# A 32-head attention's product with Wo for two token tiles at once, by seven products of sums of blocks in place of eight

## The chip, the cores and the metric

The program runs on one NeuronCore of a Trainium2 chip. TensorE (PE) multiplies matrices and writes to PSUM; VectorE (DVE), ScalarE (ACT) and GpSimd (POOL) work on tiles of 128 partitions in SBUF, the first two also on PSUM; SyncE (SP) issues the DMAs. Each engine works through its own instructions in a fixed order and waits on semaphores for the others. The metric is the device time of one execution in microseconds; less is better.

## What is computed

A block of four decoder layers on 16 x 64 tokens of width 512, in float32. Each layer adds a cross attention and a feed-forward part to x. The change is in the attention of layer 1, which has 32 query heads of width 128 and 8 key/value heads:

```python
x = x + _L0_xattn_ref(_layernorm(x, axis=-1), ctx_4096, ...)
x = x + _L0_ffn_ref(_layernorm(x, axis=-1), ...)
x = x + _L1_xattn_ref(_layernorm(x, axis=-1), ctx_4096, ...)
...
def _L1_xattn_ref(latents, context, Wq, Wk, Wv, Wo, q_norm_w, k_norm_w):
    kv = jnp.concatenate([context, latents], axis=1)
    q = (latents @ Wq).reshape(bsz, q_len, HEADS, HEAD_DIM).transpose(0, 2, 1, 3)
    k = (kv @ Wk).reshape(bsz, kv_len, KV_HEADS, HEAD_DIM).transpose(0, 2, 1, 3)
    v = (kv @ Wv).reshape(bsz, kv_len, KV_HEADS, HEAD_DIM).transpose(0, 2, 1, 3)
    q = rms_norm(q, q_norm_w)
    k = rms_norm(k, k_norm_w)
    ...
    probs = jax.nn.softmax(scores.astype(jnp.float32), axis=-1).astype(q.dtype)
    out = jnp.einsum('bhgqk,bhkd->bhgqd', probs, v)
    ...
    return out @ Wo
```

Wo is 4096 x 512. Taken by key/value head, its share is 512 x 512: four query heads of 128 rows each.

## The kernel before

**Tokens, groups, heads.** The 1024 tokens are eight tiles of 128. `groups` pairs them: (0,1), (2,3), (4,5), (6,7). x stays in SBUF for the whole program, a 128x512 tile for each token tile.

**Two lanes on one TensorE.** `decoder_kernel` writes two streams of steps and `merged` weaves them. The main lane (a) runs layer 1's attention, `normed_attention`, for all four groups, and then the rest for tiles 4 to 7. The side lane (b) runs layer 0 (window attention and an int8 FFN) for one group after the other, ahead of the main lane, and then the rest for tiles 0 to 3. Each step yields a cost in microseconds; after a main step the side lane is advanced until it has used that cost times a rate (0.85 for the first group, then 0.78, 0.78, 0.74). A `Need` makes the main lane wait, in the order of writing, until the side lane has passed a mark. TensorE runs in exactly the order written (`manual_schedule`); the order on the other engines is made by the compiler. A side step may contain no matmul at all.

**The attention as a pipeline.** `normed_attention` first makes the keys and values of the context for all heads and saves them in DRAM. Then `ticks` walks over 64 units: a unit is u = (n, t), with n = 8 x group + key/value head and t one of the group's two tiles, so that the two tiles of a head are neighbours. In tick i every step is run, in the order of the list, on the unit that lies its lag behind:

```python
(2, scores, 0.9),
(1, scale, 0.0),
(5, project, 3.4),
(0, queries, 3.4),
(1, turn, 0.7),
(0, keys_values, 1.7),
(4, values, 0.9),
(3, turn_weights, 0.4),
```

`queries` (L857) makes a unit's four query heads, `keys_values` (L875) its own keys and values, whose squares are reduced on VectorE to r, raised to the power -1/2 on GpSimd (L123). `scale` (L898) and `turn` make normed, transposed queries and keys; `scores` (L672) the products, their maximum on VectorE (L682), the exponentials on ScalarE (L688), and p divided by its sum on GpSimd (L697). `turn_weights` transposes p (copied out of PSUM on VectorE, L704), and `values` (L713) multiplies by v; ScalarE copies the result to aT, 128 x (four heads x 128 tokens) (L927). `project` multiplies the four 128x128 pieces of aT by the four 128x512 pieces of the head's Wo, adds them up in one PSUM bank (L722), and VectorE adds that bank to x (L157).

**Weights.** Head n's Wo piece, 1 MB, is loaded by `out_weights` (L761) from `queries` of head n+2, into one of two buffers of tag "o"; the buffers serve the context's key and value weights before that (`pair_weights`). The rest of the head's weights, 1.5 MB, is another load (L752).

**PSUM.** Each lane has four banks in rotation. A tick of the attention takes eight: scores, project, queries, two in `turn`, keys_values, values, turn_weights.

**The window attention of the side lane.** For each pair of tiles, `output` forms sixteen products of weights and values on VectorE (pv, L466), whose weights come by DMA from DRAM, 512 KB each (att, tag "prod"), and adds them up on GpSimd (acc, L476); it has no matmul. Its result goes into a product on TensorE (ps_o, L321).

## Time and profile before

| | us |
|---|---|
| three runs | 1639.91, 1640.31, 1640.88 (median 1640.31) |
| span of the profiled execution | 1642.0 |
| first attention unit's Wo product, last one's | 224.6, 1109.4 |
| Wo product of layer 1, TensorE busy (512 matmul instructions) | 231.1 |
| queries of layer 1, TensorE busy (512) | 233.0 |
| keys and values of layer 1, TensorE busy (512) | 125.0 |
| Wo loads, issue to landing, median (32 of 1024 KB) | 5.2 |
| transfers in all | 200.32 MB, 122 GB/s over the span |

TensorE was granted 0.993 of its full clock. The three runs lie within 0.97 us, and the profiled execution's span is 1.7 us above their median. In the profile a float32 product appears as two matmul instructions. Times of single instructions are in microseconds from the span's start; a row of a timeline gives start, length, engine, line, operation, what is written and read, shapes and how many instructions are merged in the row; brackets give idle time before it and what ended it. In the groups, the number after the bar is the time in which the engine was busy with them, then the mean length of one in ns, then the idle time before them.

### The profile page before, as it was taken

What the parts mean: (1) busy time and instruction counts of PE and PEld (TensorE: products, weight loads), DVE (VectorE), ACT (ScalarE), POOL (GpSimd) and SP (SyncE); (2) the same over time, 40 slices, a digit from 0 to 9 for tenths busy, and PEclk for the clock granted to TensorE, in tenths of its full rate; (3) what the DMA queues carried; (4) which work ended last, traced back from release to release, by engine and by line L of the source; (5) the groups of instructions that cost most, each with busy time, mean ns of one, the idle gap of its engine ahead of it and who ended that gap; (6) DMA issues with size and microseconds to landing.
All of it is one profiled execution on the core that took longest, in us unless ns stands there. A gap on an engine that the chain in (4) does not pass through costs nothing.

```text
span 1642.0 us, 20849 instructions
## 1 busy us (share of the span) xinstructions
PE 1590.8 (97%) x7104; PEld 918.9 (56%) x7104; DVE 962.6 (59%) x2000; ACT 614.7 (37%) x1929; POOL 506.2 (31%) x523
## 2 busy tenths in 40 slices
PE   7999899899999999999999999999999999999999
PEld 1334456465555645666655565554566566556774
DVE  6686588566687567776964365338246333522335
ACT  3333354334443444434443454221244332223442
POOL 1493238522385313853322132012022101011112
PEclk9999999999999999999999999999999999999999
DMA  8982359523693346943633222022220101301120
GB/s 259 272 261 82 109 164 257 177 87 120 190 279 118 109 139 176 271 162 107 231 119 126 102 74 97 29 109 73 72 71 20 46 20 49 96 29 42 39 71 26
DMA packets 98329, 200.32 MB, mean 122 GB/s; under 512 B 48945, under 2 KB 66097, under 8 KB 86449
## 3 DMA queue, kind: packets, MB, share of 16 engines
q1 hardware_dynamic: 98224, 199.00, 39.1%
q8 instruction: 57, 0.93, 0.2%
q14 instruction: 48, 0.39, 0.1%
HBM read 179.57 MB, written 19.40 MB: 121 GB/s over the span
## 4 chain that ended last, share of the span: by engine, by line
PE 80%; DVE 10%; DMA 4%; ACT 3%; POOL 2%; issue 1%; SPq 0%; ACTq 0%; POOLq 0%; DVEq 0%
PE ps_wo L722 15%; PE ps_q L857 10%; PE ps_ckv L809 7%; PE ps_kv L875 5%; PE ps_q L1462 5%; PE ps_s L672 4%; PE ps_a L713 4%; PE ps_o L1313 3%; PE ps_h L1288 3%; PE ps_pT L141 3%; DMA att<-att_d 3%; PE ps_v L1409 3%; PE ps_k L1446 2%; PE ps_dot L390 2%; PE ps_wo L1203 2%; PE ps_q L1135 2%
## 5 line engine op out<-in xcount | busy, mean ns | idle before, releaser
L722 PE MATMUL ps_wo<-l1a_o,aT 128*128 128x512 f32 x512 | 231.1, 594 | 3.1 <-ACT aT L927 3.1
L857 PE MATMUL ps_q<-l1a_w,kvT 128*128 128x512 f32 x512 | 233.0, 598 | 0.0
L688 ACT ACTIVATE p<-ps_s,mx 128x128 f32<-128x128 f32 x384 | 135.4, 369 | 211.2 <-DVE mx L683 192.4
L697 POOL TENSOR_TENSOR p<-p,sm 128x512 f32<-128x512 f32 x96 | 103.7, 1080 | 337.3 <-DVE sm L696 303.0
L123 POOL TENSOR_TENSOR r<-r,mhalf 128x5 f32<-128x5 f32 (+1 forms) x96 | 102.9, 1072 | 294.6 <-DVE r L799 280.4
L857 PEld LDWEIGHTS ps_q<-l1a_w,kvT 128*128 128x128 f32 x512 | 96.4, 192 | 117.5 <-issue 116.1
L722 PEld LDWEIGHTS ps_wo<-l1a_o,aT 128*128 128x128 f32 x512 | 92.7, 190 | 100.8 <-issue 96.3
L157 DVE TENSOR_TENSOR x<-x,ps_wo 128x512 f32<-128x512 f32 x104 | 70.6, 679 | 115.2 <-PE ps_wo L722 83.0
L875 PE MATMUL ps_kv<-l1a_w,kvT 128*128 128x256 f32 x512 | 125.0, 388 | 1.1 <-DVE x L157 0.9
L476 POOL TENSOR_TENSOR acc<-acc,pv 128x512 f32<-128x512 f32 x96 | 122.0, 1295 | 4.7 <-DVE pv L466 4.0
L809 PE MATMUL ps_ckv<-l1a_kv,kvT 128*64 128x512 f32 x512 | 116.9, 599 | 0.0
L798 DVE TENSOR_REDUCE r<-sq 128x5 f32<-128x640 f32 x64 | 52.3, 817 | 109.9 <-ACT sq L883 109.9
L123 POOL TENSOR_TENSOR rs<-rs,mhalf 128x1 f32<-128x1 f32 x64 | 36.7, 578 | 259.1 <-DVE rs L132 225.1
L875 PEld LDWEIGHTS ps_kv<-l1a_w,kvT 128*128 128x128 f32 x512 | 94.2, 194 | 18.6 <-issue 4.2
L865 ACT ACTIVATE sq<-ps_q 128x512 f32<-128x512 f32 x64 | 38.2, 597 | 158.3 <-PE ps_q L857 158.2
L466 DVE TENSOR_TENSOR pv<-att,ps_v 128x512 f32<-128x512 f32 x128 | 82.1, 676 | 22.1 <-DMA att<-att_d 18.8
L672 PE MATMUL ps_s<-kT,qT 128*128 128x128 f32 (+1 forms) x704 | 92.1, 276 | 0.1
L369 DVE TENSOR_TENSOR prod<-qs,kp 128x1024 f32<-128x1024 f32 x64 | 79.0, 1272 | 15.4 <-ACT qs L350 7.4
L704 DVE COPY pT<-ps_pT 128x512 f32<-128x512 f32 x96 | 64.3, 683 | 39.3 <-PE ps_pT L141 39.2
L672 PEld LDWEIGHTS ps_s<-kT,qT 128*128 128x128 f32 (+1 forms) x704 | 85.0, 192 | 3.4 <-issue 2.1
L1462 PE MATMUL ps_q<-kvT,l3a_w 128*128 128x256 f32 x384 | 85.6, 379 | 0.0
L722 PE MATMUL ps_wo<-l3a_o,aP 128*128 128x512 f32 x192 | 85.5, 593 | 0.0
(193 smaller groups left out, 2720.8 us busy)
## 6 DMA issues: line engine op xcount, KB each, us to landing
l1a_w<-in_l1a_w SPq DMA_DIRECT2D x32, 1536.0 KB, 7.0
att<-att_d SPq DMA_DIRECT2D x64, 512.0 KB, 9.2
l1a_o<-in_l1a_w SPq DMA_DIRECT2D x32, 1024.0 KB, 5.2
s<-ckv SPq DMA_DIRECT2D x32, 256.0 KB, 3.9
l3a_w<-in_l3a_w SPq DMA_DIRECT2D x6, 1024.0 KB, 5.2
l3a_o<-in_l3a_w SPq DMA_DIRECT2D x8, 768.0 KB, 4.3
l1a_kv<-in_l1a_kv SPq DMA_DIRECT2D x4, 1024.0 KB, 7.2
dots_d<-dots SPq DMA_DIRECT2D x16, 256.0 KB, 2.0
```

The source lines that it names most:

```text
L123: self.nc.gpsimd.tensor_tensor(out, v, self.k.mhalf[:, : v.shape[1]], ALU.pow)
L369: nc.vector.tensor_tensor(prod, bc(qs, 1, 2), spaced(kp, b * NB + j + 2 * w, [[2, 2], [1, D]]), ALU.mult,)
L466: nc.vector.tensor_tensor(pv.rearrange("p (q w n) -> p q w n", w=2, n=L), att[:, a, :].rearrange("p (q w n) -> p q w n", w=2, n=L), spaced ...
L476: nc.gpsimd.tensor_tensor(sums, before, pv, ALU.add)
L672: nc.tensor.matmul(ps[:, i, :], lhsT=qT[:, i // 2, 2 * (i % 2) : 2 * (i % 2) + 2, :].rearrange("p g s -> p (g s)"), rhs=kTs[i // 2], start ...
L688: nc.scalar.activation(p[:, i, :], ps[:, i, :], AF.Exp, bias=mx[:, i : i + 1], scale=self.scale, accum_out=sm[:, i : i + 1],)
L697: nc.gpsimd.tensor_tensor(p, p, bc(sm, 2, P), ALU.mult)
L722: self.nc.tensor.matmul(ps, lhsT=a, rhs=wo[:, g, :], start=g == 0, stop=g == len(chunks) - 1)
L809: nc.tensor.matmul(ps[j * S : (j + 1) * S], lhsT=k.context(c, 2 * t + 1 - j), rhs=w_pair[hp][:, c, :], start=c == 0, stop=c == NC - 1,)
L857: nc.tensor.matmul(ps, lhsT=k.stream(c, t), rhs=w_qkv[n][0][:, c, :], start=c == 0, stop=c == NC - 1,)
L875: nc.tensor.matmul(ps, lhsT=k.stream(c, t), rhs=w_qkv[n][1][:, c, :], start=c == 0, stop=c == NC - 1,)
L1462: nc.tensor.matmul(ps[:, j], lhsT=wq[:, c, (j0 + j) * P : (j0 + j + 1) * P], rhs=k.kvT[:, c, t : t + 2, 1:3, :], start=c == 0, stop=c == N ...
```

## The change

For the first group the product stays as it is. For the other three, a head's two tiles are multiplied together by Strassen's scheme. With a[0..3] the quarters of the two tiles' aT (first tile, lower and upper 256 rows of the head; second tile, the same) and the head's Wo as 2 x 2 blocks of 256 x 256, seven products of sums take the place of eight products of blocks. Each is 128 tokens x 256 x 256, two matmuls of 128 rows with 256 columns.

- `form_sums` makes the sums on the token side on GpSimd, with three adds, after `values` of the second tile: both (128x256), diff (128x512), and one in place in aT (128x512).
- `save_terms` makes the sums on the weights' side on GpSimd in the first group, after each `project`: six adds of 128x256 after the first tile's, four after the second's, and stores them in DRAM (768 and 512 KB).
- `load_terms` loads seven terms of 256 KB for a head in place of one 1 MB load: five from the saved sums, two out of Wo itself. Four are issued after the product of the previous head's second tile, three at the head's first product.
- `project` of the first tile makes products 0 to 3 in two banks, of the second tile 4 to 6 in two banks. VectorE adds each bank to acc, 7 x 256 wide, in SBUF; in the first head of a group it copies instead. After a group's last head, `finish` adds acc's parts to x with eight adds.
- The lag of `project` is 6 in place of 5, its cost 3.5 and 2.6 in place of 3.4 twice.
- The weights' buffers of tag "o" are eight of 256 KB in place of two of 1 MB, the context's weights loaded in four parts; aT holds both tiles. `dynamic_dma_scratch_size=64` is given to the program. The first definition of `queries`, which a second one of the same name replaced, is deleted.

```diff
--- before.py
+++ after.py
@@ -725,6 +725,171 @@
         self.ln.add_to(t, ps)
 
+class PairedProjection:
+
+    HALF = D // 2
+
+    def __init__(self, ln, es, pool, groups, w_in, n_kv):
+        self.ln, self.nc, self.pool = ln, ln.nc, pool
+        self.groups, self.w_in, self.n_kv = groups, w_in, n_kv
+        self.wpool = ln.pool(es, "l1o", 8)
+        self.dram = es.enter_context(
+            ln.tc.tile_pool(name="sums", bufs=1, space=bass.MemoryType.DRAM)
+        )
+        self.plain, self.saved, self.terms = {}, {}, {}
+        self.heads, self.sums = {}, {}
+        self.acc = None
+
+    def block(self, name):
+        return self.wpool.tile([P, D], F32, tag="o", name=name)
+
+    def is_first(self, n):
+        return n < self.n_kv
+
+    def plain_weights(self, n):
+        if n < 0 or not self.is_first(n) or n in self.plain:
+            return
+        self.plain[n] = []
+        for g in range(4):
+            w = self.block(f"l1a_o{n}")
+            self.nc.sync.dma_start(w, self.w_in[n, :, g * D : (g + 1) * D])
+            self.plain[n].append(w)
+
+    def save_terms(self, n, part):
+
+        nc, H = self.nc, self.HALF
+        w = [g.rearrange("p (j n) -> p j n", j=2) for g in self.plain[n]]
+        out = self.pool.tile([P, 3 - part, 2, H], F32, tag="acc", name="terms", bufs=1)
+        for c in range(2):
+            if part == 0:
+                for i, (a, b, op) in enumerate(
+                    [
+                        (w[c][:, 0], w[2 + c][:, 1], ALU.add),
+                        (w[c][:, 1], w[2 + c][:, 1], ALU.subtract),
+                        (w[2 + c][:, 0], w[c][:, 0], ALU.subtract),
+                    ]
+                ):
+                    nc.gpsimd.tensor_tensor(out[:, i, c, :], a, b, op)
+            else:
+                for i in range(2):
+                    g = w[2 * i + c]
+                    nc.gpsimd.tensor_tensor(out[:, i, c, :], g[:, 0], g[:, 1], ALU.add)
+        for i, m in enumerate((0, 2, 3) if part == 0 else (5, 6)):
+            saved = self.dram.tile([P, D], F32, tag=f"t{n}_{m}", name=f"t{n}_{m}")
+            nc.sync.dma_start(saved, out[:, i].rearrange("p c n -> p (c n)"))
+            self.saved[n, m] = saved
+
+    def load_terms(self, n, ms):
+        if n >= self.n_kv * len(self.groups):
+            return
+        for m in ms:
+            w = self.block(f"l1a_t{n}")
+            h = n % self.n_kv
+            if m in (1, 4):
+                i = 0 if m == 1 else 1
+                rows = self.w_in[h, :, 2 * i * D : 2 * (i + 1) * D]
+                self.nc.sync.dma_start(
+                    w.rearrange("p (c n) -> p c n", c=2),
+                    rows.rearrange("p (c n) -> p c n", c=2)[:, :, i * self.HALF : (i + 1) * self.HALF],
+                )
+            else:
+                self.nc.sync.dma_start(w, self.saved[h, m])
+            self.terms[n, m] = w.rearrange("p (c n) -> p c n", c=2)
+
+    def place(self, u):
+        n, t = u
+        first = t == self.groups[n // self.n_kv][0]
+        if first:
+            self.heads[n] = self.pool.tile([P, 2, 4, P], F32, tag="aT", name="aT")
+        return self.heads[n][:, 0 if first else 1]
+
+    def form_sums(self, u):
+
+        n, t = u
+        if self.is_first(n) or t == self.groups[n // self.n_kv][0]:
+            return
+        nc = self.nc
+        a = self.heads[n].rearrange("p t (k c) n -> p (t k) (c n)", k=2)
+        diff = self.pool.tile([P, 2, self.HALF], F32, tag="diff", name="diff", bufs=1)
+        both = self.pool.tile([P, self.HALF], F32, tag="both", name="both", bufs=1)
+        nc.gpsimd.tensor_tensor(both, a[:, 0], a[:, 3], ALU.add)
+        nc.gpsimd.tensor_tensor(diff, a[:, 2:4], a[:, 0:2], ALU.subtract)
+        nc.gpsimd.tensor_tensor(a[:, 1:3], a[:, 1:3], a[:, 0:4:3], ALU.add)
+        self.sums[n] = [
+            s.rearrange("p (c n) -> p c n", c=2)
+            for s in (both, a[:, 2], a[:, 0], a[:, 3], a[:, 1], diff[:, 0], diff[:, 1])
+        ]
+
+    def project(self, u):
+        n, t = u
+        i = self.groups[n // self.n_kv].index(t)
+        if self.is_first(n):
+            ps = self.ln.bank([P, D], "ps_wo")
+            for g in range(4):
+                self.nc.tensor.matmul(
+                    ps,
+                    lhsT=self.heads[n][:, i, g],
+                    rhs=self.plain[n][g],
+                    start=g == 0,
+                    stop=g == 3,
+                )
+            self.ln.add_to(t, ps)
+            self.save_terms(n, i)
+            if n == self.n_kv - 1 and i == 1:
+                self.load_terms(n + 1, range(4))
+            return 3.4
+        if i == 0:
+            self.load_terms(n, range(4, 7))
+        if n % self.n_kv == 0 and i == 0:
+            self.acc = self.pool.tile([P, 7, self.HALF], F32, tag="acc", name="acc", bufs=1)
+        for ms in ((0, 1), (2, 3)) if i == 0 else ((4, 5), (6,)):
+            ps = self.ln.bank([P, len(ms), self.HALF], "ps_wo")
+            for j, m in enumerate(ms):
+                for c in range(2):
+                    self.nc.tensor.matmul(
+                        ps[:, j],
+                        lhsT=self.sums[n][m][:, c],
+                        rhs=self.terms[n, m][:, c],
+                        start=c == 0,
+                        stop=c == 1,
+                    )
+            acc = self.acc[:, ms[0] : ms[-1] + 1]
+            if n % self.n_kv == 0:
+                self.nc.vector.tensor_copy(acc, ps)
+            else:
+                self.nc.vector.tensor_tensor(acc, acc, ps, ALU.add)
+        if i == 1:
+            self.load_terms(n + 1, range(4))
+            if n % self.n_kv == self.n_kv - 1:
+                self.finish(n)
+        return 3.5 if i == 0 else 2.6
+
+    def finish(self, n):
+        H, m = self.HALF, self.acc
+        one, two = (
+            self.ln.k.x[t].rearrange("p (j n) -> p j n", j=2)
+            for t in self.groups[n // self.n_kv]
+        )
+        for x, terms, op in [
+            (one, m[:, 0:4:2], ALU.add),
+            (one, m[:, 3:5], ALU.add),
+            (one[:, 0], m[:, 4], ALU.subtract),
+            (one[:, 0], m[:, 6], ALU.subtract),
+            (two, m[:, 1:3], ALU.add),
+            (two, m[:, 3:6:2], ALU.add),
+            (two[:, 1], m[:, 0], ALU.add),
+            (two[:, 1], m[:, 1], ALU.subtract),
+        ]:
+            self.nc.vector.tensor_tensor(x, x, terms, op)
+
 def normed_attention(ln, groups, rates, w_in, w_kv, norms):
 
@@ -755,32 +920,7 @@
                     w[:, NQ:].rearrange("p (c n) -> p c n", c=NC),
                 )
 
-        def out_weights(n):
-            if n >= 0 and n not in w_o:
-                w = wpool.tile([P, G * D], F32, tag="o", name=f"l1a_o{n}")
-                nc.sync.dma_start(w, w_in[n % NKV, :, NQ + NKVW :])
-                w_o[n] = w.rearrange("p (g n) -> p g n", g=G)
-
...
+        out = PairedProjection(ln, es, pool, groups, w_in[:, :, NQ + NKVW :], NKV)
 
         dram = es.enter_context(
             ln.tc.tile_pool(name="saved", bufs=1, space=bass.MemoryType.DRAM)
@@ -789,9 +929,11 @@
 
         def pair_weights(hp):
             if hp < NKV // 2 and hp not in w_pair:
-                w = wpool.tile([P, NC * 4 * HD], F32, tag="o", name=f"l1a_kv{hp}")
-                nc.sync.dma_start(w, w_kv[hp])
-                w_pair[hp] = w.rearrange("p (c n) -> p c n", c=NC)
+                w_pair[hp] = []
+                for c in range(NC):
+                    w = out.block(f"l1a_kv{hp}")
+                    nc.sync.dma_start(w, w_kv[hp, :, c * 4 * HD : (c + 1) * 4 * HD])
+                    w_pair[hp].append(w)
 
         def factors(r, sq):
 
@@ -809,7 +951,7 @@
                     nc.tensor.matmul(
                         ps[j * S : (j + 1) * S],
                         lhsT=k.context(c, 2 * t + 1 - j),
-                        rhs=w_pair[hp][:, c, :],
+                        rhs=w_pair[hp][c],
                         start=c == 0,
                         stop=c == NC - 1,
                     )
@@ -840,8 +982,7 @@
             if t == groups[n // NKV][0]:
                 qkv_weights(n)
                 qkv_weights(n + 1)
-                out_weights(n - 2)
-
+                out.plain_weights(n - 2)
 
             kT = pool.tile([P, 4, S], F32, tag="kT", name="kT", bufs=3)
             v = pool.tile([P, 2, HD], F32, tag="v", name="v", bufs=6)
@@ -923,15 +1064,13 @@
         def values(u):
             d = kept[u]
             ps = at.values(d.pop("pT"), d.pop("v"))
-            aT = pool.tile([P, G, 2, S], F32, tag="aT", name="aT")
-            nc.scalar.copy(aT.rearrange("p g b s -> p b g s"), ps)
-            d["aT"] = aT
+            aT = out.place(u)
+            nc.scalar.copy(aT.rearrange("p g (b s) -> p b g s", b=2), ps)
+            out.form_sums(u)
+            kept.pop(u)
 
         def project(u):
-            n, t = u
-            out_weights(n)
-            aT = kept.pop(u)["aT"]
-            at.project(t, [aT[:, g].rearrange("p b s -> p (b s)") for g in range(G)], w_o[n])
+            return out.project(u)
 
         pair_weights(0)
         yield Need(1, 0.95)
@@ -945,7 +1084,7 @@
             [
                 (2, scores, 0.9),
                 (1, scale, 0.0),
-                (5, project, 3.4),
+                (6, project, 3.4),
                 (0, queries, 3.4),
                 (1, turn, 0.7),
                 (0, keys_values, 1.7),
@@ -1756,7 +1895,7 @@
     import concourse.bacc as bacc
     from concourse.bass_utils import run_bass_kernel_spmd
 
-    nc = bacc.Bacc("TRN2", target_bir_lowering=False, num_devices=1)
+    nc = bacc.Bacc("TRN2", target_bir_lowering=False, num_devices=1, dynamic_dma_scratch_size=64)
     arrays, args = {}, {}
     for name, a in laid_out(inputs).items():
         arrays[f"in_{name}"] = a
```

More of the change, by code (lines that the diff above doesn't have):

```diff
@@ L756, in qkv_weights @@
                 )
-        def out_weights(n):
-            if n >= 0 and n not in w_o:
-                w = wpool.tile([P, G * D], F32, tag="o", name=f"l1a_o{n}")
-                nc.sync.dma_start(w, w_in[n % NKV, :, NQ + NKVW :])
-                w_o[n] = w.rearrange("p (g n) -> p g n", g=G)
-        def queries(u):
-            n, t = u
-            if t == groups[n // NKV][0]:
-                qkv_weights(n)
-                qkv_weights(n + 1)
-                out_weights(n - 2)
-            ps = ln.bank([P, G, HD], "ps_q")
-            for c in range(NC):
-                nc.tensor.matmul(
-                    ps,
-                    lhsT=k.stream(c, t),
-                    rhs=w_qkv[n][0][:, c, :],
-                    start=c == 0,
-                    stop=c == NC - 1,
-                )
-            sq = pool.tile([P, 6, HD], F32, tag="sq", name="sq", bufs=1)
-            nc.scalar.activation(sq[:, 0:4, :], ps, AF.Square)
-            qn = pool.tile([P, G, HD], F32, tag="qn", name="qn")
-            nc.scalar.copy(qn, ps)
-            kept[u] = dict(sq=sq, qn=qn)
+        out = PairedProjection(ln, es, pool, groups, w_in[:, :, NQ + NKVW :], NKV)
         dram = es.enter_context(
@@ L842, in queries @@
                 qkv_weights(n + 1)
-                out_weights(n - 2)
+                out.plain_weights(n - 2)
             kT = pool.tile([P, 4, S], F32, tag="kT", name="kT", bufs=3)
@@ L925, in values @@
             ps = at.values(d.pop("pT"), d.pop("v"))
-            aT = pool.tile([P, G, 2, S], F32, tag="aT", name="aT")
-            nc.scalar.copy(aT.rearrange("p g b s -> p b g s"), ps)
-            d["aT"] = aT
+            aT = out.place(u)
+            nc.scalar.copy(aT.rearrange("p g (b s) -> p b g s", b=2), ps)
+            out.form_sums(u)
+            kept.pop(u)
         def project(u):
-            n, t = u
-            out_weights(n)
-            aT = kept.pop(u)["aT"]
-            at.project(t, [aT[:, g].rearrange("p b s -> p (b s)") for g in range(G)], w_o[n])
+            return out.project(u)
         pair_weights(0)
```

## The prediction

> **What bounds the kernel now.** I read the busy shares first, then the waits of TensorE, then the costliest groups, then the timelines of one stretch of the attention.

> ```profile
> PE 1590.8 (97%) x7104; PEld 918.9 (56%) x7104; DVE 962.6 (59%) x2000; ACT 614.7 (37%) x1929; POOL 506.2 (31%) x523
> ...
> PE ps_qT L141 <- DVE qn L898: 4.6, 3, 2.1
> ...
> PE ps_wo L722 <- ACT aT L927: 3.1, 3, 2.2
> ```

> TensorE is the bound: 97% busy, and the largest waits inside the attention come to a few microseconds in 64 units of work. Two things follow: a microsecond of matmul taken away is a microsecond won, and a new wait in TensorE's fixed order is lost in full, for no other idle time is there to absorb it.

> ```profile
> L722 PE MATMUL ps_wo<-l1a_o,aT 128*128 128x512 f32 x512 | 231.1, 594 | 3.1 <-ACT aT L927 3.1
> L875 PE MATMUL ps_kv<-l1a_w,kvT 128*128 128x256 f32 x512 | 125.0, 388 | 1.1 <-DVE x L157 0.9
> L157 DVE TENSOR_TENSOR x<-x,ps_wo 128x512 f32<-128x512 f32 x104 | 70.6, 679 | 115.2 <-PE ps_wo L722 83.0
> L476 POOL TENSOR_TENSOR acc<-acc,pv 128x512 f32<-128x512 f32 x96 | 122.0, 1295 | 4.7 <-DVE pv L466 4.0
> ...
> L573 POOL TENSOR_SCALAR qT<-qT 128x512 f32<-128x512 f32 x16 | 10.0, 636 | 14.7 <-ACT qT L572 14.5
> ...
> L573 POOL TENSOR_SCALAR qT<-qT 128x256 f32<-128x256 f32 x8 | 3.2, 399 | 11.8 <-ACT qT L572 11.7
> ```

> The Wo product is the first row: 64 units (a head of one token tile) of 4 products, each two matmul instructions, so 8 to a unit. Next, one tick of the attention on TensorE, then on ScalarE and GpSimd:

> ```profile
> 670.46 3.60 PE L857 MATMUL ps_q<-l1a_w,kvT 128*128 128x512 f32 x8
> ...
> 674.44 1.89 PE L875 MATMUL ps_kv<-l1a_w,kvT 128*128 128x256 f32 x8
> 676.17 1.03 PE L713 MATMUL ps_a<-pT,v 128*128 128x256 f32 x4
> 677.04 0.60 PE L141 MATMUL ps_pT<-ident,p 128*128 128x128 f32 x4
> 677.47 1.06 PE L672 MATMUL ps_s<-kT,qT 128*128 128x128 f32 x8
> 678.37 3.60 PE L722 MATMUL ps_wo<-l1a_o,aT 128*128 128x512 f32 x8
> ...
> 677.26 0.58 ACT L927 COPY aT<-ps_a 128x512 f32<-128x512 f32 x1
> ...
> 677.94 1.18 POOL L123 TENSOR_TENSOR r<-r,mhalf 128x5 f32<-128x5 f32 x1
> 679.09 1.27 POOL L476 TENSOR_TENSOR acc<-pv 128x512 f32<-128x512 f32 x1
> ```

> After the values product come four transposes and the scores, then the Wo product. aT is copied by 677.84 and the Wo product starts at 678.37: 0.53 us to spare.

> **The matmuls removed.** A matmul's printed length contains its drain, so spacing is (stretch minus one length) over the steps: (3.60 - 0.594)/7 = 0.429 us for 512 columns, (1.89 - 0.388)/7 = 0.215 for 256. A head of two tiles now takes 16 x 0.429 = 6.86 us; seven products of two 128-row chunks, two instructions each, take 28 x 0.215 = 6.02 (0.216 unrounded: 6.05). That saves 0.82 us, in 24 heads (three groups of eight) **19.6 us**. If the spacing were as poor as the groups' busy time makes it (231.1/512 = 0.451 against 125.0/512 = 0.244), it would be 7.22 - 6.83 = 0.39 us, 9.3 us in all. I take 19.6, since L875 has the same 256 columns with new weights each time.

> [...]

> **The new wait.** Before a head's first product, GpSimd must add its sums: one add of 128x256 and two of 128x512, the second tile's aT among their inputs. That tile's values product is in tick v+4, and the product of the head's first tile (lag 6, one unit earlier) in tick v+5: the very gap shown above. The extra lag is spent on waiting for the second tile, not for the sums. The first product needs the first add, the second product the third add.

> Costs: 1.27 us for each wide add (row L476, 679.09); the narrow one is not shown, so between 0.64 (half) and 0.81 (half with the fixed part of L573: 399/636 of 1.27); I take 0.70. Together 3.24. ScalarE's end to GpSimd's start 0.17, and 0.22 from GpSimd's end to a matmul (both from such hand-overs in the timeline at 805 and 829 us). TensorE would have reached the second product 4 x 0.216 = 0.86 after the start. With s to spare, TensorE waits 0.17 + 3.24 + 0.22 - 0.86 - s = 2.77 - s: **2.24 us at s = 0.53**. If GpSimd is in an operation, its rest is added: above, r runs to 679.12, and the wait would be 3.35.

> I did this for the 24 second tiles of the three groups. s is between 0.44 and 0.65 in 17, 0.05 in two (the drain at the end), 0.92 to 2.15 in five, where side work lies in the gap. Sums: 19.5, 18.9 and 18.2 us by group, **56.6 us**. Low end 40, with the shortest rows for the adds (1.05, 0.60) and hand-overs of 0.10. High end 82, if each r traced before the sums also stands before them in GpSimd's queue: in the second group r starts up to 3.7 us after aT, and those waits become 7 us. Behind the sums on GpSimd stand r and the scaling of p; r feeds a transpose some 7 us later, so nothing more is late.

> [...]

> **The output phases of window attention.** In three stretches the side work is bound by GpSimd and by transfers:

> ```profile
> 253.50:307.30 53.80, 49.87 (x192) 29.78 (x190) 41.73 (x68) 20.85 (x74) 44.91 (x37) 0.99 0.97 246
> 449.70:503.40 53.70, 51.58 (x195) 31.73 (x194) 42.17 (x74) 20.90 (x77) 45.61 (x38) 0.97 0.96 261
> 652.90:705.00 52.10, 52.10 (x210) 32.79 (x209) 42.11 (x71) 21.91 (x81) 44.58 (x37) 1.00 1.04 286
> ```

> (Columns: PE, PEld, DVE, ACT, POOL busy, clock, DMA share, GB/s.) GpSimd is busy 45 of 54 us, the DMA engines practically always. The first lies in the plain group, where save_terms adds 10 narrow sums (7.0 us) and 1.25 MB of stores a head; about 2.35 heads pass (two ticks of 11.4 us each, 670.03 to 681.4), so 16.5 us on GpSimd against 9 us idle, and 2.9 MB, 12 us at 246 GB/s. TensorE already waits 1.5 us there for acc. I take **10 us**, between 0 (the stretch has hidden room) and 16. In the other two, 0.75 MB more a head are 1.8 MB, 6 to 7 us, mostly under the 2.35 x 2.2 us that TensorE now stands still: **2 us** (0 to 6).

> **VectorE and banks.** Two adds of 0.679 a head become three and a narrow one, some 1.1 us more, 26 us over the three groups, and eight adds (at most 8 x 0.68 = 5.4 us) close each group; VectorE is 59% busy, which hides both, except where evictions are late already (around 790 to 825 us TensorE just meets them). A unit takes nine of the lane's PSUM banks instead of eight, so the queries now wait for pT's eviction: **3 us** (0 to 10). Without that cover all 42 us could show. Term loads have a tick's lead, like the Wo load; the smaller scratch setting has nothing in this program to act on: 0. The returned costs are 0.7 lower a head, which moves side work later and removes none: 0.

> **Sum:** -19.6 + 56.6 + 10 + 2 + 3 = +52.0 on the profiled execution's own 1642.0 us gives 1694.0; the runs' median is 1.7 below its span, so **1692.3 us**.

> **Rivals.**
> - *Sums hidden* (faster). Side steps fall into the gap between values and the Wo product; from 2.8 us of TensorE work there the wait is nil. Then -19.6 + 15 - some 11 of output-phase cost that proves hidden, about 1625. For it: five of 24 gaps have such work. Against: 17 have none, and the order of TensorE is fixed. 7%.
> - *GpSimd's order*: sums behind late r, 82 in place of 57: 1692 + 25 = 1717. For it: r is traced first; against: that order is not visible here. 18%.
> - *Transfers become the bound*: all 25 us of added traffic in the three phases appear (12 + 6.5 + 6.5) in place of the 12 counted: 1705. For: DMA shares of 0.96 to 1.04; against: TensorE's own new pauses give them time. 12%.
> - *No saving*: the spacing of 256 columns is 0.244 within the products, 10 us less gained: 1702. For: the busy shares; against: the 0.215. 3%.

> **How the numbers follow.** The forecast has 60% and a range of its own of 1668 to 1712. Low end of the whole: 1640.3 - 19.6 + 40, nothing else, 1661. High end: 1717 plus 11 of the upper bounds, 1728. The measurement tells 0.2% (3.3 us) from no change. Faster is the first rival, less the part of it that lands near nothing (with a wait of about 0.8 a head): faster 6%, no change 2%, slower 92%.

> **What would show it.** In the changed profile: products of 256 columns 0.216 apart; TensorE's largest wait on the sums (GpSimd's both or aT), 24 times, 2 to 3.4 us, some 50 us; matmul time down by about 20; VectorE's share up by 2 to 3 points; ps_o waiting for acc near 300 us. I am wrong if that wait is under 20 us in all, if GpSimd's adds take well under 1.2 us, or if side work fills the gap in most heads.

## The result, and the profile after

| | before | after |
|---|---|---|
| median of four runs each, us | 1640.6 (1639.91 to 1643.38) | 1775.6 (1771.43 to 1777.52) |
| ratio, 95% interval | 1 | 1.0809 [1.0786, 1.0831] |
| span of the profiled execution, us | 1642.0 | 1769.6 |
| TensorE busy, us | 1590.8 | 1624.2 |
| TensorE idle (span less busy), us | 51.2 | 145.4 |
| granted clock | 0.993 | 0.959 |

The change makes the kernel 8.1% slower: 135 us, where 52 were forecast, and outside the range. The profile's first part (busy time and share of each engine), the row of the granted clock in 40 slices, and below them the largest waits of TensorE (in all, how many, longest):

```profile
PE 1624.2 (92%) x7392; PEld 1002.5 (57%) x7392; DVE 1021.4 (58%) x2072; ACT 616.4 (35%) x1929; POOL 651.8 (37%) x675
...
PEclk9999899999999999889999999989999999999999
```

```profile
PE ps_wo L856 <- POOL aT L824: 44.5, 21, 3.6
PE ps_wo L856 <- POOL both L822: 30.4, 18, 5.1
PE ps_gu L596 <- POOL qT L573: 9.7, 3, 7.9
PE ps_q L141 <- DVE xs L565: 9.3, 5, 6.3
```

Three things are to be seen. TensorE is *busier* than before by 33.4 us, although the matmuls are fewer in work: at a lower clock the same product takes longer (an instruction of L856: 634 ns in the median from 719.4 to 723.0, at clock 0.50, and 379 from 512.9 to 515.2, at 1.00). The waits on the sums come to 74.9 us. And two waits of layer 0's feed-forward (L596, L141), in which the change edits no instruction, have grown: 9.7 from 3.9 and 9.3 from 1.0.

The span grew by 127.6 us: 94.2 of idle time and 33.4 of busy time. If the products save the 19.6 us of the forecast, 53 us of busy time have come in elsewhere. The clock can account for that: (1 - 0.959) x 1769.6 = 72.6 us lost to it, against 11.5 before, is 61 us more (a little too much, since it counts half clock in pauses as well, as the 0.50 from 717.08 to 719.48 below, where no matmul runs). One tick shows both losses. TensorE's timeline (start, length, what is done; in brackets the idle time before it and what ended it), GpSimd's for the same time, and three stretches of it (columns: length; PE, PEld, DVE, ACT, POOL busy; clock, DMA share, GB/s):

```profile
712.60 1.06 PE L672 MATMUL ps_s<-kT,qT 128*128 128x128 f32 x8
715.90 1.18 PE L856 MATMUL ps_wo<-l1a_t,both 128*128 128x256 f32 x4 [2.24 <-POOL both L822]
719.48 4.91 PE L856 MATMUL ps_wo<-l1a_t,aT 128*128 128x256 f32 x12 [2.41 <-POOL aT L824]
724.23 3.60 PE L998 MATMUL ps_q<-l1a_w,kvT 128*128 128x512 f32 x8
```

```profile
713.91 1.25 POOL L426 TENSOR_TENSOR dots<-dots,sm 128x512 f32<-128x512 f32 x1 [2.02 <-ACT v L1029]
715.13 0.72 POOL L822 TENSOR_TENSOR both<-aT 128x256 f32<-128x256 f32 x1
715.81 1.26 POOL L823 TENSOR_TENSOR diff<-aT 128x512 f32<-128x512 f32 x1
717.03 1.17 POOL L123 TENSOR_TENSOR r<-r,mhalf 128x5 f32<-128x5 f32 x1
718.17 1.26 POOL L824 TENSOR_TENSOR aT<-aT 128x512 f32<-128x512 f32 x1
```

```profile
713.00:717.00 4.00, 1.76 (x10) 1.14 (x9) 3.97 (x9) 1.42 (x6) 3.09 (x3) 0.98 1.02 292
717.00:724.00 7.00, 4.59 (x12) 3.68 (x12) 3.82 (x5) 1.51 (x8) 5.14 (x5) 0.52 0.99 288
724.00:730.00 6.00, 6.00 (x24) 3.79 (x23) 4.38 (x7) 1.83 (x4) 1.68 (x2) 1.00 1.02 298
```

TensorE waits twice, 4.65 us in all against the 2.24 that the prediction worked out for such a gap. Three things lengthen the wait here. The copy of aT itself comes late: TensorE has ended the scores at 713.66, ScalarE the copy at 714.46.

```profile
713.87 0.59 ACT L1068 COPY aT<-ps_a 128x512 f32<-128x512 f32 x1
```

Then an operation of window attention (`dots`) stands ahead of the sums, and r stands between the second and the third. Right after the first pause the clock falls to half, 0.50 for 6.83 us from 716.85 on. The twelve products at 719.48 are then (4.91 - 0.49)/11 = 0.40 us apart instead of 0.216, and the clock is back for the queries at 724.23. So the wait is paid for a second time.

### The profile page after: what moved, and what is told of

The parts are those of the page before. It is cut to its first block, busy times and chain, and to the rows that moved or that the text cites. A ratio compares the mean times of both kernels' runs of the same rounds, so it can differ in the third digit from the quotient of the medians.

```text
span 1769.6 us, 22060 instructions
## 1 busy us (share of the span) xinstructions
PE 1624.2 (92%) x7392; PEld 1002.5 (57%) x7392; DVE 1021.4 (58%) x2072; ACT 616.4 (35%) x1929; POOL 651.8 (37%) x675
## 4 chain that ended last, share of the span: by engine, by line
PE 67%; POOL 12%; DVE 11%; DMA 5%; ACT 3%; issue 2%; SPq 0%; POOLq 0%; ACTq 0%; DVEq 0%
PE ps_wo L856 8%; PE ps_q L998 8%; PE ps_wo L722 5%; PE ps_q L1601 4%; PE ps_kv L1016 4%; PE ps_ckv L951 4%; PE ps_o L1452 3%; PE ps_s L672 3%; PE ps_a L713 3%; PE ps_v L1548 2%; PE ps_h L1427 2%; PE ps_k L1585 2%; PE ps_pT L141 2%; POOL terms L779 2%; PE ps_gu L596 2%
## 5 line engine op out<-in xcount | busy, mean ns | idle before, releaser
L123 POOL TENSOR_TENSOR r<-r,mhalf 128x5 f32<-128x5 f32 (+1 forms) x96 | 102.5, 1068 | 233.7 <-DVE r L941 230.7
L856 PE MATMUL ps_wo<-l1a_t,aT 128*128 128x256 f32 x384 | 127.6, 492 | 44.5 <-POOL aT L824 44.5
L123 POOL TENSOR_TENSOR rs<-rs,mhalf 128x1 f32<-128x1 f32 x64 | 36.5, 575 | 281.9 <-DVE rs L132 265.8
L856 PEld LDWEIGHTS ps_wo<-l1a_t,aT 128*128 128x128 f32 x384 | 92.4, 251 | 71.1 <-POOL aT L824 53.6
L476 POOL TENSOR_TENSOR acc<-acc,pv 128x512 f32<-128x512 f32 x96 | 123.1, 1304 | 15.9 <-DVE pv L466 15.8
L157 DVE TENSOR_TENSOR x<-x,ps_wo 128x512 f32<-128x512 f32 x56 | 38.2, 682 | 94.2 <-PE ps_wo L722 53.3
L867 DVE TENSOR_TENSOR acc<-acc,ps_wo 128x512 f32<-128x512 f32 x84 | 50.7, 613 | 72.4 <-PE ps_wo L856 72.3
L672 PE MATMUL ps_s<-kT,qT 128*128 128x128 f32 (+1 forms) x704 | 91.6, 276 | 0.0
L466 DVE TENSOR_TENSOR pv<-att,ps_v 128x512 f32<-128x512 f32 x128 | 81.5, 677 | 14.3 <-POOL acc L476 6.2
L369 DVE TENSOR_TENSOR prod<-qs,kp 128x1024 f32<-128x1024 f32 x64 | 82.8, 1335 | 8.4 <-ACT qs L350 3.8
L672 PEld LDWEIGHTS ps_s<-kT,qT 128*128 128x128 f32 (+1 forms) x704 | 85.1, 192 | 3.6 <-issue 2.4
L722 PE MATMUL ps_wo<-l3a_o,aP 128*128 128x512 f32 x192 | 85.5, 593 | 0.0
```

Of the source, the lines that this page charges most:

```text
L123: self.nc.gpsimd.tensor_tensor(out, v, self.k.mhalf[:, : v.shape[1]], ALU.pow)
L369: nc.vector.tensor_tensor(prod, bc(qs, 1, 2), spaced(kp, b * NB + j + 2 * w, [[2, 2], [1, D]]), ALU.mult,)
L466: nc.vector.tensor_tensor(pv.rearrange("p (q w n) -> p q w n", w=2, n=L), att[:, a, :].rearrange("p (q w n) -> p q w n", w=2, n=L), spaced ...
L476: nc.gpsimd.tensor_tensor(sums, before, pv, ALU.add)
L672: nc.tensor.matmul(ps[:, i, :], lhsT=qT[:, i // 2, 2 * (i % 2) : 2 * (i % 2) + 2, :].rearrange("p g s -> p (g s)"), rhs=kTs[i // 2], start ...
L722: self.nc.tensor.matmul(ps, lhsT=a, rhs=wo[:, g, :], start=g == 0, stop=g == len(chunks) - 1)
```

## The experiments

All times are medians; ratios are to the kernel before, run on the same chip. Idle is span less TensorE's busy time; clock loss is (1 - granted clock) x span. The last four columns belong to the one profiled execution, which lies up to 4.4 us from its kernel's median. Each median is of 2 to 12 runs. The kernel before has medians from 1639.0 to 1642.0 us on the chips used, so a difference between times of two rows is good to some 3 us.

| kernel | time, us | ratio, 95% interval | span | busy | idle | clock loss |
|---|---|---|---|---|---|---|
| before | 1640.6 | | 1642.0 | 1590.8 | 51.2 | 11.5 |
| after | 1775.6 | 1.0809 [1.0786, 1.0831] | 1769.6 | 1624.2 | 145.4 | 72.6 |
| wait1 | 1681.9 | 1.0255 [1.0225, 1.0284] | 1678.8 | 1597.5 | 81.3 | 15.1 |
| wait3 | 1797.0 | 1.0957 [1.0925, 1.0988] | 1796.5 | 1642.9 | 153.6 | 75.5 |
| no_save | 1734.1 | 1.0573 [1.0544, 1.0602] | 1731.8 | 1615.4 | 116.4 | 57.2 |
| late | 1687.5 | 1.0290 [1.0262, 1.0317] | 1685.5 | 1590.2 | 95.3 | 43.8 |
| warm | 1757.6 | 1.0715 [1.0676, 1.0754] | 1757.4 | 1653.8 | 103.6 | 33.4 |
| late_no_save | 1647.8 | 1.0067 [1.0030, 1.0105] | 1645.9 | 1577.7 | 68.2 | 23.0 |
| late_hold | 1679.3 | 1.0254 [1.0222, 1.0286] | 1672.8 | 1586.9 | 85.9 | 26.8 |
| nostore | 1673.3 | 1.0189 [1.0133, 1.0245] | 1671.8 | 1589.8 | 82.0 | 30.1 |
| spread | 1668.3 | 1.0161 [1.0118, 1.0204] | 1664.8 | 1584.7 | 80.1 | 21.6 |
| act_evict | 1647.8 | 1.0041 [1.0019, 1.0062] | 1642.7 | 1578.7 | 64.0 | 19.7 |
| products | 1620.4 | 0.9879 [0.9860, 0.9898] | 1615.9 | 1567.7 | 48.2 | 8.1 |
| products7 | 1636.3 | 0.9973 [0.9960, 0.9986] | 1637.0 | 1576.9 | 60.1 | 21.3 |

**The wait alone, put into the kernel before** (wait3: adds of 256, 512 and 512 columns on GpSimd between values and the Wo product; wait1: the last alone, by `(D,)`). The scratch setting of the change comes along, for room.

```diff
             nc.scalar.copy(aT.rearrange("p g b s -> p b g s"), ps)
+            if u[0] >= NKV and u[1] == groups[u[0] // NKV][1]:
+                flat = aT.rearrange("p g b s -> p (g b s)")
+                for w in (D // 2, D, D):
+                    nc.gpsimd.tensor_tensor(flat[:, :w], flat[:, :w], zero[:, :w], ALU.add)
```

> The kernel before, with three GpSimd adds of zeros (128x256, 128x512, 128x512) put between the copy of aT and the Wo product for the second tile of each head in the last three groups; the products stay as they were. Theory A (a pause of TensorE costs its own length and then a stretch at half clock): 24 waits of 0.17 + 3.24 + 0.22 - 0.53 = 3.1 us, 70 to 75 us, and some 20 half-clock stretches that cost 40 to 55 us more: 1750 to 1770 us, clock about 0.96. Rival B (the low clock belongs to the products of 256 columns or to the added traffic): 1710 to 1716 us, clock 0.99.

> As the run with three adds, but one add of 128x512: waits of 0.17 + 1.27 + 0.22 - 0.53 = 1.1 us, 24 to 27 us in all. Theory A: in the traces so far the shortest single pause followed by a half-clock stretch is about 2 us, so few or no stretches more than before: 1662 to 1675 us, clock 0.985 or above. Rival (any new pause of a microsecond lowers the clock): 1700 us or more.

wait3 got 1797 us, above what either theory said, and the clock of the changed kernel, 0.958, without one product of 256 columns in Wo and without new traffic. So neither of those is needed for the low clock: with the pauses put in it fell from 0.993 to 0.958. The pauses themselves were longer than expected, 4.6 us on the mean instead of 3.1, since other work of GpSimd stands in the way there too: in the head below, r was still running when TensorE reached the gap at 667.07, and the three adds took 3.80 us. Waits and timeline of wait3, one head with its pause and the next unit without, and GpSimd in that pause:

```profile
PE ps_wo L722 <- POOL aT L934: 109.3, 24, 7.5
```

```profile
671.32 5.40 PE L722 MATMUL ps_wo<-l1a_o,aT 128*128 128x512 f32 x8 [4.25 <-POOL aT L934]
...
684.49 3.70 PE L722 MATMUL ps_wo<-l1a_o,aT 128*128 128x512 f32 x8
```

```profile
666.33 1.17 POOL L123 TENSOR_TENSOR r<-r,mhalf 128x5 f32<-128x5 f32 x1 [8.41 <-DVE r L801]
667.46 3.80 POOL L934 TENSOR_TENSOR aT<-aT,zero 128x256 f32<-128x256 f32 x3
```

The same eight products take 1.70 us more after the pause. In wait1 the pauses add up to a third and the clock hardly falls (0.991), as Theory A has it, so its 41 us are mostly idle time (+30.1 idle, +6.7 busy):

```profile
PE ps_wo L722 <- POOL aT L934: 37.6, 22, 5.5
```

The waits are more than the 24 to 27 us expected, and the time lies above the 1675. The premise that no single pause under some 2 us had been followed by half clock was also too strong: in the changed kernel's trace one of 1.44 us was (at 1185.98).

**Without the weights' sums.** `self.save_terms(n, i)` is taken out; the terms come out of Wo as it lies.

> The changed kernel without save_terms: the weights' sums are neither made nor stored, and the terms are loaded from Wo itself, with the same number and size of loads; the sums of Wo are left out of the computation. Theory A: the 18 us that are lost before the first attention unit and some 8 to 12 us in the first group go, with the half-clock stretches there; the sums' wait stays: 1740 to 1752 us. Rival C (the early loss comes from the loads in four parts or another order of engines): 1765 us or more.

It gained 41.5 us, a little more than expected, with the waits on the token sums as they were (43.8 + 30.6 against 74.9). Where the 41.5 lay: the compiler had put the weights' sums of the first two heads far ahead of their place in the text. GpSimd and TensorE of the changed kernel, before the first attention unit:

```profile
128.96 4.35 POOL L779 TENSOR_TENSOR terms<-l1a_o,l1a_o 128x256 f32<-128x256 f32 x6 [2.48 <-DMA l1a_o<-in_l1a_w]
...
135.60 2.77 POOL L783 TENSOR_TENSOR terms<-l1a_o 128x256 f32<-128x256 f32 x4 [1.64 <-DMA t<-terms]
138.34 0.56 POOL L123 TENSOR_TENSOR rs<-rs,mhalf 128x1 f32<-128x1 f32 x1
```

```profile
143.77 2.03 PE L141 MATMUL ps_q<-ident,xs 128*128 128x128 f32 x8 [6.31 <-DVE xs L565]
```

GpSimd stands still for a Wo load and for its own store, adds for 7 us, and only then reaches rs, which layer 0's feed-forward needs: TensorE waits 6.3 us. The first queries come at 193.9 us instead of 175.9; without the weights' sums at 176.9. So 17 us are lost before the attention begins. At the second group's first queries the two kernels are 36.2 us apart (411.2 and 375.0), so nearly all the rest is lost in the first group.

**Token sums one tick earlier than their use.** The lag of `project` is 7, and a head's sums are formed after the previous head's last product (`next_sums` calls `form_sums` for head n+1):

```diff
+                self.next_sums(n)
...
-            out.form_sums(u)
...
-                (6, project, 3.4),
+                (7, project, 3.4),
```

> The changed kernel with the token sums made a tick earlier than they are needed: project has lag 7, and a head's sums are issued after the previous head's second product. Theory A: the waits on the sums (75 us) go, and with them the half-clock stretches after 480 us (17 of them, about 50 us): 1640 to 1660 us. Rival B (clock low because of the 256-column products or traffic): 1695 to 1705 us, clock still below 0.97 after 480 us. Rival C (term loads late): waits on DMA appear.

No wait on the token sums is left, and 88 us are gone, but 1687.5 is not 1640 to 1660. The same sums are still made and the 256-column products still run, yet between 480 and 1240 us the clock is 0.98, where the changed kernel has 0.94: rival B falls. The early loss stayed (first queries at 192.1), and TensorE now meets waits on VectorE's work (pT, qn, acc):

```profile
PE ps_q L141 <- DVE xs L565: 14.0, 4, 9.0
PE ps_dn L632 <- POOL qT L573: 11.3, 3, 5.6
PE ps_gu L596 <- POOL qT L573: 9.1, 3, 6.7
PE ps_q L1005 <- DVE pT L704: 8.2, 3, 4.2
...
PE ps_qT L141 <- DVE acc L871: 4.8, 1, 4.8
```

**The pauses filled with useless work.** Three products of 512 columns of the identity with a term, into a bank of their own, ahead of each head's first products, in the changed kernel:

```diff
+        if i == 0:
+            ps = self.ln.bank([P, D], "ps_warm")
+            for j in range(3):
+                self.nc.tensor.matmul(ps, lhsT=self.ln.k.ident, rhs=..., start=True, stop=True)
```

> The changed kernel with three products of 128x128x512 (six matmul instructions, 6 x 0.429 = 2.6 us) of no use put on TensorE ahead of each head's first product, in the place where it waits for the sums; nobody reads what they give. They fill most of a wait of 3.1 us and add work. Theory A (an idle TensorE loses its clock, a waiting one does not lose anything else): the half-clock stretches after 480 us mostly go, the wait that is left is 0.5 to 1 us a head, and the time falls although TensorE has 62 us more to do: 1725 to 1745 us. Rival (the stretches come from something else than the pauses, or are as many): 1775 us or more.

TensorE has some 62 us more to do and the kernel is 18 us *faster* than the changed one: idle time fell by 41.8 and the clock loss by 39.2. 28.7 us of waits for the third add were left, in 17 pieces, hence 1757.6 and not 1725 to 1745. The clock is thus a cost of its own, that work in the pause takes away.

**Both losses removed.** late with no_save's edit.

> Both parts at once: sums a tick earlier (lag 7), and no save_terms (the sums of Wo are left out of the computation). If the two losses are independent: 1687 - 41 = 1646 us, the rest of the early loss gone, and what is left against 1640.3 - 19.6 = 1621 are waits on VectorE (25 us in the run with early sums) and what they do to the clock. If they overlap: 1655 us or more.

As expected: 40 us below late, the same as no_save's 41.5 below after. The two losses are independent. But with neither wait left it is still above the kernel before.

**Where the weights' sums may stand.** late_hold keeps the compiler from moving them forward; nostore is late_hold without the 40 stores; spread puts one add at a time at five places of a tick, each held there.

```diff
-            self.save_terms(n, i)
+            with self.ln.tc.issue_after(self.ln.last_of(mybir.EngineType.Pool)):
+                self.save_terms(n, i)
```

> Sums a tick earlier (lag 7), and save_terms kept behind the GpSimd instruction that was traced last before it, so that the compiler cannot pull it forward into layer 0's work; everything is computed. Theory A: the 18 us before the first attention unit come back, the 10 us of the first group's output phase do not: 1655 to 1665 us. If it was not the place in GpSimd's queue but the stores or the loads of save_terms: 1680 us or more.

> The run with early sums and held save_terms, without the 40 stores of the sums (10 MB); the adds on GpSimd stay, the terms are loaded from Wo (the sums of Wo are left out of the products). Between it and the run without save_terms (1648 us) lie the adds alone, between it and the held run (1679 us) the stores. Theory A (GpSimd's queue: chains of six and four adds stand ahead of layer 0's short operations): 1670 us or more. Rival (the stores in a phase where the DMA engines are full): 1655 us or less.

> The run with early sums, the weights' sums made one add at a time, each held behind the GpSimd instruction that was traced last, at five places of a tick from the tick after the load on; stores as before, everything computed. Theory A (what stands ahead of a short operation costs, not the work itself): an operation of layer 0 waits for one or two adds (0.7 to 1.4 us) in place of six (4.3 us): 1655 to 1668 us. Rival (the amount of work on GpSimd, or the stores): 1675 to 1685 us, as held.

Holding brings back the early 17 us (first queries at 175.3) but gains only 8 in all, so 1679.3 misses the 1655 to 1665: the adds now stand ahead of layer 0's work in the first group. GpSimd of late_hold, and TensorE's largest wait, 9.9 us long, of which the six adds are 4.1:

```profile
337.18 4.12 POOL L779 TENSOR_TENSOR terms<-l1a_o,l1a_o 128x256 f32<-128x256 f32 x6
341.28 1.20 POOL L573 TENSOR_SCALAR qT<-qT 128x512 f32<-128x512 f32 x2
```

```profile
PE ps_gu L596 <- POOL qT L573: 11.3, 2, 9.9
```

By the medians the stores are worth 6.0 us (not resolved: the two intervals overlap), the adds 25.5 (nostore against late_no_save). Adds and stores together cost 31.5 when held in chains (late_hold against late_no_save) and 20.5 when spread out. spread is the best of the kernels here that compute the whole, and is 1.6% slower than before.

**Where the saving went.** Two theories for late_no_save's missing 27 us were tried. act_evict copies the products' banks out on ScalarE instead of adding them up on VectorE:

```diff
-            if n % self.n_kv == 0:
-                self.nc.vector.tensor_copy(acc, ps)
-            else:
-                self.nc.vector.tensor_tensor(acc, acc, ps, ALU.add)
+            self.nc.scalar.copy(acc, ps)
```

> The run with early sums and without save_terms, in which ScalarE copies each bank of products into acc in place of VectorE's copy or add (the sums of Wo and the adding up over heads are left out of the computation); finish stays on VectorE. It asks what the 27 us are that the run without it (1648 us) lies above 1640.3 - 19.6 = 1621. Theory A (VectorE's queue, longer by some 40 us of adds, lets TensorE wait for banks and for qn, and the clock falls behind those waits): 1624 to 1634 us, the waits on VectorE's acc and pT under 8 us in all. Rival (the 256-column products do not give the 19.6 us): 1640 us or more.

1647.8 again, on the rival's side. TensorE's waits on acc went from 11.2 us to 1.4 (then on ScalarE's copies) and the time did not follow, so VectorE's accumulation is not it; the waits on pT, 9.0 before, are 12.0. Then no sums at all, with the project step at its place in the changed kernel (lag 6) and one tick later (lag 7):

```diff
-        nc.gpsimd.tensor_tensor(both, a[:, 0], a[:, 3], ALU.add)
-        nc.gpsimd.tensor_tensor(diff, a[:, 2:4], a[:, 0:2], ALU.subtract)
-        nc.gpsimd.tensor_tensor(a[:, 1:3], a[:, 1:3], a[:, 0:4:3], ALU.add)
...
-            for s in (both, a[:, 2], a[:, 0], a[:, 3], a[:, 1], diff[:, 0], diff[:, 1])
+            for s in (a[:, 0], a[:, 2], a[:, 0], a[:, 3], a[:, 1], a[:, 1], a[:, 2])
```

> No sums at all: the seven products take the quarters of aT as they are and blocks of Wo as they lie (GpSimd forms nothing, nothing is stored), the project step at its place in the changed kernel, VectorE copying and adding the products as there. The outputs of groups 2 to 4 are then not the product with Wo. Theory A (the products do save 19.6 us, and what late_no_save and act_evict lost was idle time and clock around other waits that come with a step put one tick later): TensorE's busy time about 1572 at full clock, time 1621 to 1632. Rival B (the packed products' arrangement itself, with its accumulation on VectorE and the end of each group, costs what it saves): 1637 to 1650.

> The kernel without any sums, with the project step one tick later, as in late_no_save. If the later place is what costs (it moves the projection and its accumulation past the side lane's work): 1638 to 1648, 10 us or more above the kernel without sums at the earlier place. If not: within 4 us of it, and the adds themselves, on GpSimd, would be what late_no_save paid for.

These two settle whether the products save: by themselves they save 20 us (ratio 0.9879, busy time down by 23.1, of which 3.4 is a better clock), so act_evict's rival falls. They carry the added loads of terms too (219.27 MB in all against 200.32), and TensorE's waits on those loads come to 0.6 us. The groups of products and of the changed kernel, side by side in that order:

```profile
L851 PE MATMUL ps_wo<-l1a_t,aT 128*128 128x256 f32 x672 | 153.7, 380 | 1.0 <-DMA l1a_t<-in_l1a_w 0.6 <-ACT v L1024 0.3
```

```profile
L856 PE MATMUL ps_wo<-l1a_t,aT 128*128 128x256 f32 x384 | 127.6, 492 | 44.5 <-POOL aT L824 44.5
```

In the changed kernel this group's shortest instructions take 379 ns and its longest 796: 492 is the mean of some at full and some at half clock. One tick later, products7 loses 15.9 us of the saving, and late_no_save, which differs from it only in the token sums, another 11.5.

## Why the prediction was wrong, point by point

By differences between these kernels, the 135 us are: **-20.2** the seven products (products less before), **+113.7** the token sums at their place (no_save less products), **+41.5** the weights' sums (after less no_save). They are differences of medians from several chips; with each kernel taken against the kernel before on its own chip they are -20.7, 115.8 and 39.9. The forecast had -19.6, 56.6 and 10, and 5 for the rest.

**The step that failed first: the new wait was priced as idle time alone.** The sum has no term for the clock. From products to no_save the span grows by 115.9 us: 68.2 of idle time and 47.7 of busy time, with the same products in both. So some 40% of what the token sums cost is TensorE at half speed after the pause. The profile before had shown it, in a stretch whose clock of 0.97 the text quotes (449.70 to 503.40): a pause of the size that the forecast worked out, and behind it eight products that took 3.66 us instead of the 1.89 of 674.44. After a wait of 5.0 us, eight query products took 5.44 instead of 3.60:

```profile
455.35 0.63 PE L141 MATMUL ps_qT<-ident,qn 128*128 128x128 f32 x4 [2.09 <-DVE qn L898]
...
456.12 3.66 PE L875 MATMUL ps_kv<-l1a_w,kvT 128*128 128x256 f32 x8
```

```profile
175.03 1.11 PE L141 MATMUL ps_xT<-ident,xn 128*128 128x128 f32 x4 [5.00 <-DVE rs L132]
175.93 5.44 PE L857 MATMUL ps_q<-l1a_w,kvT 128*128 128x512 f32 x8
```

That is some 1.8 us on top of a pause of 2.1. Not every such pause brought it: of that trace's four single pauses of 2.1 us two were followed by half clock and two (at 523.58 and 642.10) were not. Even at that rate 24 pauses cost some 20 us more, an estimate. The text quoted clocks of 0.97 to 1.00 and drew nothing from them.

**The wait itself was mis-sized**: 74.9 us against 56.6 (bounds 40 to 82), in 39 pieces. Where GpSimd is free, the working, 2.77 - s for each head, comes out only some 0.3 to 0.6 us too long; the two hand-overs, 0.17 and 0.22 us in the sum, are 0.08 and 0.05 in the changed kernel. In 16 of 24 heads r or another operation stood ahead of the sums, as the second rival had it, and in 7 one stood between the adds, as at 717.03 above, which neither foresaw. In two heads the copy of aT came after TensorE was free, where the forecast has a spare s of at least 0.05. The place on TensorE was right: the gap between values and the first product.

**The weights' sums were mis-sized by four, and put in the wrong place.** The forecast costed them in the first window-attention output phase, at GpSimd's idle share and the DMA rate there. Its sign, TensorE waiting for acc near 300 us, hardly came: ps_o waits 2.0 us. Of the 41.5 us, 17 were lost before the attention begins and most of the rest in the first group, where layer 0's feed-forward waits for short operations of GpSimd (ps_gu for qT between 230 and 446 us: 8.5 us, none without the weights' sums). A queue that is busy for 31% of the span was taken to have room; what counted was what stood right behind the new work. The stores, which the forecast weighed at 12 us, were worth some 6 in late_hold.

**VectorE and banks** stayed within their bounds of 0 to 10 in the changed kernel, where the waits on acc are 0.6 us and none is on pT: as the text said, there is cover. With the pauses gone (late), waits of 25 us appear on VectorE's pT, qn and acc, inside the bound of 42. In act_evict the accumulation is gone from VectorE and the time is the same, so it is not what makes late_no_save slow.

**What was right**: the saving (19.6 forecast, 20.2 measured, so the rival without a saving falls); the sign; that transfers do not bind, as far as the loads of terms go (products has them and saves 20 us all the same).

**Not settled**: why the projection one tick later costs 15.9 us. products7 has 11.9 us more idle time than products and 9.2 more busy time, in small waits on GpSimd's qT (ps_gu: 6.7 against 1.1) and on VectorE; which step is displaced was not tried. Nor was a place for the token sums found that leaves the 20 us standing.

## What to carry to other kernels

Price a new wait on a saturated TensorE by its idle time and by the half clock that can follow it (in the traces here behind 33 of 56 lone pauses of 2 to 3 us), and read both from a pause that the trace already holds; here a saving of 0.8 us a head that put a pause of some 3 us into it was given back several times over. For work added to a queue that is mostly idle, ask at each place which short operation stands right behind it and who waits for that, and whether the compiler may move the new work forward to where it waits for a load. Before building such a change whole, run its saving alone (here: products without sums) and its wait alone (here: adds of zero in the kernel before, which cost even more than the sums in their place, 156 us against 113.7).

## What the runs showed of the hardware

| pause, us | 0.5 to 1 | 1 to 1.5 | 1.5 to 2 | 2 to 3 | 3 and more |
|---|---|---|---|---|---|
| pauses | 121 | 93 | 33 | 56 | 51 |
| half clock after it | 0 | 5 | 8 | 33 | 50 |

So half clock began in or behind 83 of the 107 pauses of 2 us or more, and 13 of the 247 shorter ones. What decides it for a single pause was not shown.

**GpSimd's add and VectorE's operations at the same time.** In 14 of 24 heads of the changed kernel the 128x512 add into diff took 1.71 to 1.81 us instead of 1.26 to 1.28, each time with a VectorE operation on two SBUF tiles under way as it began; in the other ten there was none. VectorE and GpSimd of the changed kernel:

```profile
1059.90 0.68 DVE L1039 TENSOR_TENSOR qn<-qn,r 128x512 f32<-128x512 f32 x1
1060.51 1.28 DVE L1040 TENSOR_SCALAR kn<-kn,r 128x128 f32<-128x128 f32 x1
```

```profile
1059.92 1.79 POOL L823 TENSOR_TENSOR diff<-aT 128x512 f32<-128x512 f32 x1
```

GpSimd's add starts 0.02 us after qn and takes 0.52 us longer, close to qn's 0.68; kn then takes 1.28 instead of 0.28 (the median of L1040) and ends 0.08 us after the add. So in this head half a microsecond more is on GpSimd's add and one on VectorE's kn; what holds the two up was not shown.
